# Layers 2 and 3 of a four-layer graph network run as one flow on one Trainium2 core, with the input check's reads of the adjacency moved behind layer 1's end

## The chip, the core and the metric

The kernel runs on one core of a Trainium2 chip (trn2). The metric is the device time of the program in microseconds (us); lower is better. A profile is one more execution, recorded by the hardware; its span is the time between its first and last recorded instruction.

## What is computed

The reference sends 4096 nodes with 64 features each through four graph layers, with a normalisation ahead of each layer and a residual sum behind it. The adjacency matrix is 4096 x 4096, float32, with entries 0 or 1 (an edge with probability about 1/128, and the diagonal). Layer 0 is graph attention with eight heads and an output layer, layer 1 is hyperbolic attention. Cut to what the change touches, the rest is:

```python
h = relu(layernorm(x))                       # ahead of each layer
# layer 2: mean over the neighbours and the node, joined to the node itself
agg = (adj @ h + h) / max(deg + 1, 1)
z = relu(concat([h, agg]) @ W2 + b2)
x = x + z / norm(z)                          # row by row
h = relu(layernorm(x))
# layer 3: the first 100 neighbours of each node, the weight of each halved with its rank
x = x + weights(adj, 100, 0.5) @ (h @ W3) + b3
```

Layer 3's weight of an edge depends on how many edges of the same row stand beside it, so it is built from counts along each row.

## The kernel before, in words

Nodes are held in 32 blocks of 128 (tile `x` and its normalised copy `h`, [128, 32, 64]). A group is four blocks, 512 nodes; there are eight groups and two halves (`hf`) of 2048 target nodes. The edges are kept in DRAM as one byte each (`mask_d`), written earlier, and are streamed as matmul operands.

**Order of instructions.** A tile layer draws the edges between instructions and then orders each engine's queue from an estimate of its own[...]. `in_order()` pins the order inside a block as it is written. `tc.issue_after(i)` makes the instructions of its block that run on `i`'s engine stand behind `i` there; it adds no wait between engines. Loads are issued on SyncE's queue (SP), small ones on GpSimd's (POOL).

**The input check.** The fast path is valid only if every adjacency entry is 0 or 1. `count_odd` (line 946) loads one slab of the float32 adjacency, 128 x 2048 (1 MB, tile `raw`, two buffers), on SP (L949), and VectorE counts its odd entries in one pass (L950). There are 64 such slabs: 16 are counted in layer 0, 12 are traced in layer 2 (L2525) and 36 in layer 3 (L2710, nine for each of four passes). The total decides at the end (L2758 to L2763) whether the general path must be run.

**Layer 1's finish** (`finish_steps`, line 2356) is run for the two halves, interleaved by `side_by_side` (L2506) and pinned. Per half: `pvt` matmuls (L2376) sum layer 1's accumulators by node, VectorE scales them (L2380), then a long chain of VectorE operations on [128, 16, 64] tiles and on [128, 16] scalars, with ScalarE's Square, Sqrt, Tanh and Sqrt between, the residual, the normalisation (`norm_steps`), and `h` split into two half-precision parts (`HH`, L2497 to L2502).

**Layer 2.** For each half of targets, eight loads of edges (`m2`, 1 MB, three buffers) feed 16 `nacc` matmuls each (features, L2517) and 16 `dc` matmuls (degrees, L2529). At the half's end the sums are copied out (`ev`, `cf`) and four groups are finished one after another (L2552 to L2594): `pnf`, `cat`, transposes and `cT`, `pz`, `zt`, norm, residual. PSUM: five banks for sums, three for the rest. The groups of half 0 stand beside half 1's products.

**Between the layers** `layernorm_relu()` (L2597) normalises the two halves. Then layer 3's pools are opened and its constants made (L2604 to L2650: loads of W3 and b3, the triangle `tri`, `blk`, `late` from the counts, and the scaled weights), and the values `SS` (L2652 to L2666) of the eight groups: transposes, `hT`, `psup`, two half-precision parts.

**Layer 3** makes four passes (`u`) over 1024 targets each. A pass has 32 steps `j`: two `pv` matmuls with `blk` and `late` (L2691), two with `tri` and the edges (L2699), ScalarE's conversion to the weights `w3b` (L2708), and two `sacc` matmuls with `SS` (L2673), one step behind. Every four steps an edge tile `m3` (0.5 MB, three buffers, L2684) is loaded. A pass ends with `ev` (L2717, one on VectorE and one on ScalarE), `pn` (L2722) and the output. `sacc` has two banks, so the next pass's sums start once `ev` has read them.

Of the kernel before, what the change touches and what calls it, by code (L numbers as in the profile page):

```python
# [15 lines left out]
I16 = mybir.dt.int16  # L16
# [814 lines left out]
def kernel(  # L831
# [127 lines left out]
    def norm_steps(bs, wide, tag, act=True):  # L959
# [4 lines left out]
        mean = small("ln_mean", nb)  # L964
# [11 lines left out]
        var = small("ln_var", nb)  # L976
# [1379 lines left out]
    def finish_steps(hf, VQ, VT, fold_v, pabs, wide, ps):  # L2356
# [41 lines left out]
        f, rpm = scal("finf"), scal("rpm")  # L2398
        nc.vector.tensor_scalar(f, pm[:, bs], hrow, None, ALU.mult)
        nc.vector.tensor_tensor(f, f, pc[:, bs], ALU.mult)  # L2400
        nc.vector.reciprocal(rpm, pm[:, bs])
        nc.vector.tensor_tensor(g, g, ab, ALU.mult)
        nc.vector.tensor_tensor(xu, xu, g, ALU.subtract)
        nc.vector.tensor_tensor(xu, xu, f, ALU.mult)
        uu, un, arg = scal("uu"), scal("un"), scal("arg")
        nc.vector.tensor_reduce(uu, t, AX.X, ALU.add)
        nc.vector.tensor_tensor(uu, uu, f, ALU.mult)
        nc.vector.tensor_tensor(uu, uu, f, ALU.mult)
# [3 lines left out]
        nc.vector.tensor_scalar(un, un, sqc, None, ALU.mult)  # L2412
        nc.vector.tensor_tensor(arg, rpm, un, ALU.mult)
        nc.scalar.activation(arg, arg, AF.Tanh)
        yield True

        nc.vector.reciprocal(un, un)
        nc.vector.tensor_tensor(arg, arg, un, ALU.mult)
# [5 lines left out]
        nc.vector.tensor_tensor(den, ab, uu, ALU.mult)  # L2424
        nc.vector.scalar_tensor_tensor(den, den, c2, one2, ALU.mult, ALU.add)
# [3 lines left out]
        nc.vector.tensor_scalar(den, den, MIN_NORM, None, ALU.max)  # L2429
        nc.vector.reciprocal(den, den)  # L2430
        nc.vector.tensor_tensor(pp, pp, den, ALU.mult)
        nc.vector.tensor_tensor(pp, pp, den, ALU.mult)
        nc.vector.tensor_scalar(pp, pp, MIN_NORM, None, ALU.max)
        nc.scalar.activation(pp, pp, AF.Sqrt)
        nc.vector.scalar_tensor_tensor(num, uu, cc, one2, ALU.mult, ALU.add)
        nc.vector.tensor_tensor(num, num, den, ALU.mult)
        nc.vector.tensor_tensor(arg, arg, f, ALU.mult)
        nc.vector.tensor_tensor(den, den, pc[:, bs], ALU.mult)
        nc.vector.tensor_tensor(arg, arg, den, ALU.mult)
# [3 lines left out]
        nc.vector.tensor_scalar(pp, pp, maxn, 1.0, ALU.mult, ALU.min)  # L2443
        nc.vector.tensor_tensor(num, num, pp, ALU.mult)
        nc.vector.tensor_tensor(arg, arg, pp, ALU.mult)
# [15 lines left out]
    def layers_fast(es, *sums):  # L2461
# [14 lines left out]


        with ExitStack() as l2:
            lp = l2.enter_context(tc.tile_pool(name="l2f", bufs=1))
            work = l2.enter_context(tc.tile_pool(name="l2fwork", bufs=2))  # L2480
            ps_acc = l2.enter_context(tc.tile_pool(name="ps_nacc", bufs=5, space=PSUM))
            ps = l2.enter_context(tc.tile_pool(name="ps_l2", bufs=3, space=PSUM))
            w2 = lp.tile([2 * D, D], F32, name="w2f")
            nc.gpsimd.dma_start(w2, W2)
            b2t = lp.tile([P, D], F32, name="b2f")
            nc.gpsimd.dma_start(b2t, b2.unsqueeze(0).to_broadcast([P, D]))
            sel = lp.tile([P, NB * O], BF16, name="sel")
            nc.gpsimd.memset(sel, 0.0)
            nc.gpsimd.memset(sel[:, :: O + 1], 1.0)
            HH = lp.tile([P, NB, 2, D], F16, name="HH")  # L2490
            wide = l2.enter_context(tc.tile_pool(name="finwide", bufs=3))

            def nodes(hf):
                yield from finish_steps(hf, *sums, wide, ps)
                bs = halves[hf]
                hs = wide.tile([P, HB, D], F32, name="hs", tag="fat")
                nc.scalar.activation(HH[:, bs, 0, :], h[:, bs], AF.Copy, scale=VALH)  # L2497
                yield True
                nc.vector.scalar_tensor_tensor(
                    hs, h[:, bs], VALH, HH[:, bs, 0, :], ALU.mult, ALU.subtract  # L2500
                )
                nc.scalar.activation(HH[:, bs, 1, :], hs, AF.Copy, scale=LO)  # L2502


            with in_order():
                side_by_side(nodes(0), nodes(1), 2, 10)  # L2506
            for hf in range(2):
                accs = [ps_acc.tile([P, G], F32, name="nacc", tag="nacc") for _ in range(NS)]
                dc = ps_acc.tile([P, G], F32, name="dc", tag="nacc")
                for q in range(NQ):  # L2510
# [13 lines left out]
                    if hf or q >= NQ // 2:  # L2524
                        count_odd(work, next(todo))  # L2525
# [26 lines left out]
                for g in range(NS):  # L2552
                    b0 = hf * HB + g * GB
                    bs = slice(b0, b0 + GB)
                    hg = h[:, bs, :]
                    pn = ps.tile([P, GB, D], F32, name="pnf", tag="misc")
                    for b in range(GB):
                        nc.tensor.matmul(
                            pn[:, b, :],
                            lhsT=ev[:, g, b * P : (b + 1) * P],  # L2560
                            rhs=fold_h,
                            start=True,
                            stop=True,
                        )
                    cat = work.tile([P, GB, 2 * D], F32, name="cat", tag="cat")
                    nc.gpsimd.tensor_copy(cat[:, :, 0:D], hg)
                    nc.vector.scalar_tensor_tensor(
                        cat[:, :, D:], pn, 1.0 / VALH, hg, ALU.mult, ALU.add
                    )
                    nc.vector.tensor_tensor(  # L2570
                        cat[:, :, D:], cat[:, :, D:], over(deg[:, g, :], D), ALU.mult
                    )
                    cT = work.tile([P, G], F32, name="cT", tag="cT")
                    transpose_to(cT, [cat[:, b, :] for b in range(GB)], P, ps, nc.scalar.copy)
                    pz = ps.tile([P, GB, D], F32, name="pz", tag="misc")
                    for b in range(GB):
                        nc.tensor.matmul(
                            pz[:, b, :], lhsT=cT[:, b * P : (b + 1) * P], rhs=w2, start=True, stop=True
                        )
                    zt = work.tile([P, GB, D], F32, name="zt", tag="zt")  # L2580
                    nc.vector.tensor_tensor(
                        zt, pz, b2t.unsqueeze(1).to_broadcast([P, GB, D]), ALU.add
                    )
                    nc.scalar.activation(zt, zt, AF.Relu)
                    sq = work.tile([P, GB, D], F32, name="sq2", tag="sq2")
                    nc.scalar.activation(sq, zt, AF.Square)
                    nrm = small("nrm", GB)
                    nc.vector.tensor_reduce(nrm, sq, AX.X, ALU.add)
                    nc.vector.tensor_scalar(nrm, nrm, 1e-24, None, ALU.max)
                    nc.scalar.activation(nrm, nrm, AF.Sqrt)  # L2590
                    nc.vector.reciprocal(nrm, nrm)
                    nc.vector.tensor_tensor(zt, zt, over(nrm, D), ALU.mult)
                    xg = x[:, bs, :]
                    nc.vector.tensor_tensor(xg, xg, zt, ALU.add)  # L2594


        layernorm_relu()  # L2597
        with ExitStack() as l3:
            lp = l3.enter_context(tc.tile_pool(name="l3f", bufs=1))
            work = l3.enter_context(tc.tile_pool(name="l3fwork", bufs=2))  # L2600
            ps_acc = l3.enter_context(tc.tile_pool(name="ps_sacc", bufs=2, space=PSUM))
            ps = l3.enter_context(tc.tile_pool(name="ps_l3", bufs=2, space=PSUM))
            ps_v = l3.enter_context(tc.tile_pool(name="ps_v", bufs=2, space=PSUM))
            w3 = lp.tile([D, D], F32, name="w3f")  # L2604
            nc.gpsimd.dma_start(w3, W3)
            b3t = lp.tile([P, D], F32, name="b3f")
            nc.gpsimd.dma_start(b3t, b3.unsqueeze(0).to_broadcast([P, D]))
            aft = lp.tile([P, P], F32, name="aftf")
            nc.gpsimd.affine_select(
                out=aft,  # L2610
                in_=ones,
                pattern=[[-1, P]],
                compare_op=ALU.is_gt,
                fill=0.0,
                base=0,
                channel_multiplier=1,
            )

            lat = lp.tile([P, P], BF16, name="lat")
            nc.vector.memset(lat, 0.0)  # L2620
            for q in range(4):
                qs = slice(q * O, (q + 1) * O)
                nc.vector.tensor_copy(lat[qs, qs], aft[qs, qs])

            nc.vector.tensor_scalar(aft, aft, -VBITS, None, ALU.mult)
            tri = lp.tile([P, P], BF16, name="tri")
            nc.vector.scalar_tensor_tensor(
                tri, ident, MAX_NEIGH * VBITS, aft, ALU.mult, ALU.add
            )
# [189 lines left out]
```

## Time and profile before

Three runs: 2236.69, 2244.22 and 2248.63 us, median 2244.22. The profiled execution took 2246.54 us.

| | |
|---|---|
| profiled execution, time | 2246.54 us |
| its span | 2244.6 us |
| PE busy | 1912.7 us, 85% |
| VectorE (DVE) busy | 1749.8 us, 78% |
| ScalarE (ACT) busy | 1599.9 us, 71% |
| moved by DMA | 239.01 MB, mean 106 GB/s |
| layer 1's last product sum on PE, then its finish | ends 1813.0, finish to 1890.8 us |
| layer 2's products, half 0, then half 1 | 1890.8 to 1928.8, then to 1976.5 us |
| first `ev` of layer 3 on DVE, last `ev` | 2091.5 and 2233.5 us |

How to read it: PE is TensorE's matmuls, PEld its weight loads, SPq SyncE's DMA queue. A group names the line, the engine, the operation, output and inputs, shape and count, then busy time and mean duration, then the idle time of that engine ahead of it and who ended it. A table by windows gives for each stretch of the span the busy time and count of instructions of each engine, the clock granted to TensorE as a share of full speed (PEclk), the share of time in which the DMA engines were busy, and the rate. A timeline row is start, duration, engine, line, operation, and in brackets the idle time before it and its releaser.

### The profile page before, as it was taken

The numbers are of one execution on the slowest core, as the hardware profiler recorded it, in microseconds if no ns is written. First come the engines' busy times: TensorE is split into PE (matmuls) and PEld (weight loads), VectorE is DVE, ScalarE is ACT, GpSimd is POOL, SyncE is SP. The second block draws the span as 40 slices with busy tenths as digits, with TensorE's granted clock in tenths as the row PEclk, the third lists the DMA queues.
The fourth block names the chain that finished last, engine by engine and source line by source line (L and its number), as shares of the span: only waits on it lengthen the run. The fifth ranks groups of instructions, "written<-read, shape, count | busy, mean of one in ns | idle before, by whom it ended". The sixth has DMA issues, their size and how long they took to land.

```text
span 2244.6 us, 43714 instructions
## 1 busy us (share of the span) xinstructions
PE 1912.7 (85%) x19229; PEld 872.8 (39%) x19276; DVE 1749.8 (78%) x2128; ACT 1599.9 (71%) x1347; POOL 84.6 (4%) x124
## 2 busy tenths in 40 slices
PE   4989989999999999859992699989999953959998
PEld 3444444444444444424442233333333331434332
DVE  6689989987898899798657889998999868345451
ACT  4668888996898899557753878888888911115666
POOL 1000100100000000001101000000000000000000
PEclk8999999999999999869995799999999966968999
DMA  9945554352111120367540101101110045526883
GB/s 111 183 91 105 91 90 115 124 187 98 44 63 49 40 77 2 123 227 280 191 139 3 32 28 33 33 24 33 33 33 29 24 147 175 186 78 231 297 305 104
DMA packets 117008, 239.01 MB, mean 106 GB/s; under 512 B 11059, under 2 KB 84003, under 8 KB 102051
## 3 DMA queue, kind: packets, MB, share of 16 engines
q1 hardware_dynamic: 101990, 192.92, 25.1%
q0 software_dynamic: 14816, 43.18, 10.9%
q8 instruction: 153, 2.51, 0.5%
q14 instruction: 49, 0.40, 0.1%
HBM read 245.34 MB, written 49.46 MB: 131 GB/s over the span
## 4 chain that ended last, share of the span: by engine, by line
PE 35%; DVE 16%; ACT 5%; DMA 5%; issue 4%; POOL 0%; SPq 0%; DVEq 0%; POOLq 0%; ACTq 0%
PE accj L2280 6%; PE acco L1971 4%; DMA raw<-in_adj_dram 4%; PE pu L2247 3%; PE nacc L2517 3%; DVE raw L950 3%; PE pf L2318 2%; PE pl L2216 2%; DVE at L2269 2%; PE pl L2219 2%; PE accC L1544 2%; ACT sg L2203 1%; DVE at L2274 1%; PE accB L1544 1%; PE ddo L1984 1%
## 5 line engine op out<-in xcount | busy, mean ns | idle before, releaser
L1208 ACT ACTIVATE st<-srow,nt 128x2048 int8<-128x2048 f32 x352 | 682.8, 1994 | 78.3 <-DVE B L1214 77.5
L1214 DVE TENSOR_TENSOR B<-st,mres 128x1024 int32<-128x1024 int32 x256 | 311.7, 1220 | 68.3 <-PE accC L1544 45.1
L1544 PE MATMUL accB<-B,ybh 128*32 128x512 fp8e4 x3072 | 338.9, 384 | 15.6 <-DVE B L1214 15.6
L1544 PE MATMUL accD<-B,ybh 128*32 128x512 fp8e4 x2048 | 301.1, 387 | 23.6 <-DVE h L1660 23.6
L1544 PEld LDWEIGHTS <-ybh 128*32 128x32 bf16 (+1 forms) x6656 | 196.6, 98 | 239.1 <-issue 76.9
L1544 PE MATMUL accC<-B,ycn 128*32 128x512 fp8e4 x2272 | 268.0, 381 | 1.2 <-issue 1.2
L1544 PE MATMUL accC<-mres,ych 128*32 128x512 fp8e4 x2272 | 268.3, 381 | 0.0
L1544 PE MATMUL accL<-B,ybh 128*32 128x512 fp8e4 x1536 | 220.1, 389 | 4.8 <-DVE h L1664 4.7
L2280 PE MATMUL accj<-sg,VQ 128*64 128x512 f32 (+1 forms) x512 | 200.0, 622 | 20.7 <-DVE sg L2321 9.2
L1544 PEld LDWEIGHTS <-ych 128*32 128x32 f16 x4096 | 168.8, 98 | 116.3 <-issue 11.3
L1202 DVE TENSOR_SCALAR st<-srow,nt 128x2048 uint8<-128x2048 f32 x160 | 205.4, 1284 | 2.5
L950 DVE SCALAR_TENSOR_TENSOR raw<-raw 128x2048 f32<-128x2048 f32 x64 | 146.4, 2287 | 69.6 <-DMA raw<-in_adj_dram 69.6
L2280 PE MATMUL acci<-sg,VQ 128*64 128x512 f32 (+1 forms) x512 | 199.4, 622 | 0.0
L2203 ACT ACTIVATE sg<-pl,rb 128x512 f32<-128x512 f32 x256 | 163.4, 684 | 47.7 <-PE pl L2219 32.2
L2708 ACT ACTIVATE w3b<-pv 128x1024 int16<-128x1024 f32 x128 | 131.1, 1024 | 52.2 <-PE pv L2699 51.8
L1208 ACT ACTIVATE st<-srowo,nto 128x1024 int8<-128x1024 f32 x128 | 137.3, 1138 | 40.9 <-DVE B L1214 40.7
L2247 PE MATMUL pu<-XAf,LDf 66*128 66x512 f32 x288 | 146.5, 611 | 9.1 <-DVE at L2254 7.4
L1544 PE MATMUL accC<-C,ych 128*32 128x512 fp8e4 x1824 | 146.4, 389 | 1.9 <-DVE C L1222 1.9
L1222 DVE TENSOR_TENSOR C<-B,mres 128x1024 int32<-128x1024 int32 x114 | 139.5, 1225 | 3.6
L1544 PEld LDWEIGHTS <-ycn 128*32 128x32 f16 x2272 | 107.8, 97 | 64.0 <-issue 3.2
L2254 DVE TENSOR_SCALAR at<-pu 128x512 f32<-128x512 f32 x144 | 95.2, 684 | 30.0 <-PE pu L2247 29.3
L2517 PE MATMUL nacc<-m,HH 128*128 128x512 fp8e4 x256 | 60.8, 387 | 61.8 <-ACT HH L2502 61.8
(502 smaller groups left out, 3102.5 us busy)
## 6 DMA issues: line engine op xcount, KB each, us to landing
raw<-in_adj_dram SPq DMA_DIRECT2D x64, 1024.0 KB, 6.7
mo<-edges SPq DMA_DIRECT2D x32, 512.0 KB, 4.7
noedge<-nmo POOLq DMA_DIRECT2D x32, 512.0 KB, 4.9
nm<-noedge SPq DMA_DIRECT2D x64, 256.0 KB, 3.0
m<-edges SPq DMA_DIRECT2D x16, 1024.0 KB, 4.8
m<-edges SPq DMA_DIRECT2D x32, 512.0 KB, 5.1
srow<-srow_d SPq DMA_DIRECT2D x15, 1024.0 KB, 6.6
mres<-in_adj_dram POOLq DMA_DIRECT2D x8, 1024.0 KB, 36.3
```

The costliest lines, as they stand in the source:

```text
L950: nc.vector.scalar_tensor_tensor(raw, raw, 0.0, raw, ALU.is_gt, ALU.not_equal, accum_out=bad[:, c : c + 1])
L1202: nc.vector.tensor_scalar(st[:, i, :].bitcast(U8), srow, negs[:, i : i + 1], EDGE, ALU.is_gt, ALU.mult)
L1208: nc.scalar.activation(st[:, i, :], srow, AF.Sign, bias=negs[:, i : i + 1], scale=-1.0)
L1214: nc.vector.tensor_tensor(B.bitcast(I32), st.bitcast(I32), edges.bitcast(I32), ALU.bitwise_and)
L1222: nc.vector.tensor_tensor(C.bitcast(I32), B.bitcast(I32), edges.bitcast(I32), ALU.bitwise_xor)
L1544: ins = nc.tensor.matmul(acc[k * O : (k + 1) * O, :], lhsT=values, rhs=moving(k), start=start, stop=stop,)
L2203: tc.keep_in_program_order(nc.scalar.activation(*args, **kw))
L2247: nc.tensor.matmul(pu, lhsT=LD[:, j * P : (j + 1) * P], rhs=XA[:, grp(gi)], start=True, stop=True,)
L2254: nc.vector.tensor_scalar(at[:, b, :], pu, UMIN, None, ALU.max)
L2280: nc.tensor.matmul(acc[r : r + n, :], lhsT=XQ[:, src, cols], rhs=w, start=start, stop=stop)
L2517: nc.tensor.matmul(accs[k], lhsT=HH[:, j].rearrange("p s d -> p (s d)"), rhs=m8[:, t, k * G : (k + 1) * G], start=(j == 0), stop=(j == NB ...
L2708: nc.scalar.activation(w, pv, AF.Relu)
```

## The change

It has five parts.

1. Layers 2 and 3 share pools, opened ahead of both; the shared PSUM pool `ps` has two banks and layer 2's sums six. Layer 3's loads of W3 and b3 are issued with layer 2's, and its constants are made behind layer 1's finish.
2. A group goes from layer 2's end on through its own normalisation and to its layer-3 values in one function. `late` is made for each half as soon as its groups are through; layer 3's passes follow without a stage between.
3. `count_odd` is traced 3 and 5 times in layer 2 and 7, 11, 11 and 11 times in layer 3. The counts of layer 2 stand behind layer 1's finish on VectorE, those of layer 3 behind the last group's values.
4. `finish_steps` has fewer operations on [128, 16] tiles: the factors `f`, `f2`, `kp`, `pf` and `ac2` are made once in layer 1's stage, and one clamp and several products are folded. The ScalarE steps stay.
5. `norm_steps` names its small tiles by width.

```diff
-        with ExitStack() as l2:
...
-            ps_acc = l2.enter_context(tc.tile_pool(name="ps_nacc", bufs=5, space=PSUM))
-            ps = l2.enter_context(tc.tile_pool(name="ps_l2", bufs=3, space=PSUM))
+        ps = es.enter_context(tc.tile_pool(name="ps_l23", bufs=2, space=PSUM))
...
+        ready, valued = [], []
...
+            ready.append(
                 nc.vector.scalar_tensor_tensor(
                     hs, h[:, bs], VALH, HH[:, bs, 0, :], ALU.mult, ALU.subtract
                 )
+            )
...
+        def not_before_nodes():
+            return tc.issue_after(ready[-1].ins)
+
+        with not_before_nodes():
...
+            blk = lp.tile([P, NB, P], BF16, name="blk")
+            nc.vector.tensor_scalar(blk, over(bsel, P), -VBITS, None, ALU.mult)
...
+        def layer2_group(b0, part, deg):
...
+            nc.vector.tensor_tensor(xg, xg, zt, ALU.add)
+
+            for _ in norm_steps(bs, work, "sq2"):
+                pass
+            hT = work.tile([D, G], F32, name="hT3", tag="hT3")
+            transpose_to(hT, [h[:, b, :] for b in range(b0, b0 + GB)], D, ps, nc.scalar.copy)
+            pu = ps.tile([P, GB, D], F32, name="psup", tag="misc")
...
+            nc.scalar.copy(SS[:, bs, 0, :], pu)
+            lo = work.tile([P, GB, D], F32, name="lo3", tag="lo3")
+            valued.append(nc.vector.tensor_tensor(lo, pu, SS[:, bs, 0, :], ALU.subtract))
+            nc.scalar.activation(SS[:, bs, 1, :], lo, AF.Copy, scale=LO)
...
+        with tc.tile_pool(name="ps_nacc", bufs=6, space=PSUM) as ps_acc:
             for hf in range(2):
...
-                    if hf or q >= NQ // 2:
-                        count_odd(work, next(todo))
+                    if q <= NQ // 2 if hf else q > NQ // 2:
+                        with not_before_nodes():
+                            count_odd(work, next(todo))
...
                 for g in range(NS):
...
+                    layer2_group(hf * HB + g * GB, ev[:, g, :], deg[:, g, :])
                 pl = ps.tile([P, G], F32, name="plate", tag="misc")
                 nc.tensor.matmul(pl, lhsT=lat, rhs=cnt16[:, hf], start=True, stop=True)
                 nc.vector.tensor_scalar(late[:, hf], pl, VBITS, None, ALU.min)
...
-        layernorm_relu()
...
-                        if j % 7 < 2 and j < 28 or j == 30:
-                            count_odd(work, next(todo))
+                    if j % 3 == 0 if u else j % 2 and j > NB // 2 + 1:
+                        with tc.issue_after(valued[-1].ins):
+                            count_odd(work, next(todo))
```

## The prediction

> **What bounds the kernel now.** I read the page's slices first: PE is at 0.8 or more in most of the 40, and the low ones that this change touches are the 33rd, 34th and 36th (1796 to 2020 us). Then the chain of work that ended last, in order of time, and a table by windows cut where that chain changes hands.
>
> ```profile
> core 0: us, PE busy (x) PEld busy (x) DVE busy (x) ACT busy (x) POOL busy (x), PEclk, DMA share, GB/s
> ...
> 1815.00:1830.00 15.00, 13.67 (x64) 13.51 (x64) 4.11 (x10) 0.00 (x0) 0.00 (x0) 0.52 0.82 342
> 1830.00:1890.00 60.00, 0.00 (x0) 0.00 (x0) 56.98 (x98) 12.36 (x16) 0.74 (x2) 0.50 0.52 175
> 1890.00:1929.00 39.00, 38.22 (x258) 15.10 (x259) 16.55 (x38) 5.49 (x8) 0.00 (x0) 0.95 0.53 189
> 1929.00:1977.00 48.00, 47.35 (x344) 23.96 (x342) 17.08 (x41) 7.58 (x18) 2.22 (x5) 1.00 0.37 132
> 1977.00:2005.00 28.00, 19.34 (x88) 16.97 (x88) 10.46 (x30) 6.25 (x15) 1.41 (x3) 0.54 0.00 0
> 2005.00:2025.00 20.00, 0.63 (x1) 0.14 (x2) 15.20 (x26) 2.75 (x6) 2.68 (x3) 0.50 0.50 187
> ...
> 2053.00:2092.00 39.00, 36.40 (x177) 13.10 (x179) 19.57 (x21) 28.46 (x32) 0.00 (x0) 1.00 0.86 294
> 2092.00:2143.00 51.00, 47.95 (x205) 16.18 (x209) 25.20 (x27) 33.26 (x33) 1.55 (x2) 0.90 0.83 295
> ...
> 2190.00:2234.00 44.00, 41.83 (x193) 13.69 (x197) 7.28 (x12) 32.33 (x32) 1.86 (x3) 1.00 0.34 117
> ```
>
> From 1830 to 1890 (layer 1's finish) DVE is the bound, 57 of 60 us. From 1890 to 1977 (layer 2's products) it is PE. From 1977 to 2025 PE works little and at half clock. Layer 3's passes are PE's again, but up to 2190 with the DMA engines busy 83 to 86% of the time; the last pass, which has almost no slabs to load, takes 44 us and the pass from 2092 took 51.
>
> The slabs (`raw`) show why. First the view of that tile, then the timeline of DVE:
>
> ```profile
> DMA to landing us min/median/max: 5.0/6.7/14.1
> ```
>
> ```profile
> 2061.11 2.29 DVE L950 SCALAR_TENSOR_TENSOR raw<-raw 128x2048 f32<-128x2048 f32 x1 [3.78 <-DMA raw<-in_adj_dram]
> ...
> 2070.29 2.29 DVE L950 SCALAR_TENSOR_TENSOR raw<-raw 128x2048 f32<-128x2048 f32 x1 [4.40 <-DMA raw<-in_adj_dram]
> ...
> 2080.30 2.29 DVE L950 SCALAR_TENSOR_TENSOR raw<-raw 128x2048 f32<-128x2048 f32 x1 [3.91 <-DMA raw<-in_adj_dram]
> ```
>
> These are every second count, one of the two buffers: 2.3 us on DVE, then at once the next load, about 7 us. Two buffers turn every 9 to 10 us.
>
> **The change part by part.** Times are from the profiled execution. The order of the built program's instructions says where each stands.
>
> *Layer 1's finish*, 1815.2 (last `VT` sum on DVE) to 1890.8: 75.6 us. In the new order 20 of the 32 `pvt` stand among the last pair products, and of the three groups that stand last on PE one doesn't need the last sum. A group takes 1.7 us now, at half clock (eight passes of 0.214 us). Behind the last sum remain two groups and one scaling, 2 x 1.7 + 0.4 = 3.8 us instead of 14.3. Each matmul is recorded as two passes, so the 20 moved ones are 40; at the 0.12 us of the same kind of matmul at full clock (`pnf`, 8 passes in 0.9 to 1.0 us) they are 4.8 us in a stretch where PE is busy 79 to 82%: between 0 and 4.8, I take 2. From there the chain now takes 61.3 us with 12 slab counts at 2.21 us in it, 26.5 us, all of them on a DVE that never stops. They leave. Some hid ScalarE: the count at 1881.9 lay beside Square (1.06 us), others beside Sqrt behind a table load (1.28 us). I rebuilt the chain operation by operation, 1.2 us for a wide one and 0.2 for a narrow one: 12.9 us up to the second half's `V`, 24.1 to the first half's `HH`, 37.0 in all, of which some 3.3 us are waits that come to light and 1.3 are narrow operations saved. Here the Trainium skill speaks against the removal: "ScalarE: Activation LUTs", Rules for kernel authors, says to budget about 2.7 us for every switch of table set. The new order still has five switches. At the row's 1.28 us I get 37; at 2.7 two switches would show and it would be about 40. The row decides. Sum: 2 + 3.8 + 37 = 43 us instead of 75.6, **-33**.
>
> *Layer 2, half 0*: 38 us now. PE's order has one small matmul (L2534) in the fourth quarter that needs `wsq`, and that stands on DVE behind the second half's chain and `blk` (2.2 us). PE reaches it about 42 us after `V`, DVE about 44.5: 3 us, with the nacc products queued behind. The edge loads queue on SP behind the third slab, which waits for the first count; this ends in the same 3 us. Bounds 0 and 6. **+3**.
>
> *From half 1's start to the first `ev` of layer 3*: 1928.8 to 2091.5, 162.7 us now. It consists of half 1 (48), the tail of four groups at half clock (28), the norm and the wait for W3 and the constants (20) and the first pass with values and slab waits (66). In the new kernel a group is one chain. From the rows at 1931 to 1937: `cat` to `sq` 4.8, norm and residual 2.0; with the rows of `ln_mean` and the value steps scaled to a group (0.46 for each [128,256] operation, 0.2 for a narrow one, 0.57 + 0.65 + 1.0 + 0.4 + 0.5 for transposes, `hT`, `psup`, `SS`, `lo`): norm 3.1, values 3.5. That is 13.4 us, and DVE's order has one group wholly behind the other. Half 0's four groups, 54 us, and three or four slab counts that show with 1.5 to 2.3 us each, 8 us in all, end about 62 us after half 1's start; PE has 36.3 of products and 4 x 4.2 of groups beside it, so DVE's chain, not PE, is late. Then `plate`, `pdeg`, `pnf` 2.5 us. Half 1's four groups run beside pass 0: PE's order puts about nine steps of 1.31 us and 3.8 us of the group into each, 15.6 us, and ScalarE's 1.02 us conversions stand between the chain's eight ScalarE operations. The nearest row for that is the present value stage beside pass 0: 4.5 to 5.3 us from transposes to `lo` instead of 3.5, a factor 1.3 to 1.5. On the 9 us of chain that go through PE and ACT this gives 16 to 18 us; I take 16.5, four times 66. Bounds 13.4 and 22 a group. With two counts (4.6) that stand ahead of `ev`: 62 + 2.5 + 66 + 4.6 = 135. **-27.5**. Norm, W3 and constants are in here at nothing: they lie beside half 0 and the chain.
>
> *From the first to the last `ev`*: 142 us now. Here the slabs come back. Of 48 slabs behind layer 0, 8 are counted in layer 2; DVE's order has two ahead of the first `ev`, then 11, 16 and 11. So 38 slabs instead of 23 fall into three passes, and none of them can start earlier, because both buffers are full while the chain of groups runs. Bytes: 38 x 1.049 + 21 x 0.524 + 1 = 51.8 MB. Between 2091.5 and 2198.6 the DMA queues now move 32.5 MB, 303 GB/s, so 171 us. By buffer turns: a slab landed in 5.0 us when no edge loads ran beside it (1851.6 to 1856.7) and about 7.0 with 1.75 edge loads per turn; with one per turn 6.1, and 2.4 for the count: 19 turns of 8.5 are 162. I take 167. Passes 1 to 3 on PE need 44 each, 132, and are covered. The skill's "DMA: Bandwidth & Descriptors", Bandwidth, gives 341 GB/s for transfers of 1 MB; by that it would be 152. The rows with two slabs in flight decide. **+25**.
>
> *End*: `ev` to the last record 11.1; the flag now stands ahead of the last `ev` on DVE and waits for POOL 0.5: **+1**.
>
> Sum: -33 + 3 - 27.5 + 25 + 1 = -31.5. The profiled execution's 2246.5 becomes 2215; it lay 2.3 above the median of the runs, so the forecast is **2213 us**. A difference under 0.5% (11 us) can hardly be told from none in this kernel.
>
> **The rivals.** *The transfers keep up*: if slabs land in 5 us beside edge loads too, three passes are PE's 132 to 140 us and the gain is 60: about 2183. For it: bins of over 400 GB/s, and the present passes were partly held by SP waiting for PE. Against it: 83 to 86% busy at 300 GB/s. 20%.
>
> *The group chain is slower in company*: 22 us a group, with ScalarE's and PE's queues in strict order, +22 us, and the finish uncovers 5 us more: 2240. For it: factor 1.5 above. 17%, half of it above 2233.
>
> *Slower than before*: SP's edge loads wait for PE to free a tile, slabs stand behind them, counts stand ahead of `ev` on DVE, and `ev` holds PE's next sums. If this ring runs in turn and not side by side, each of three pass ends costs PE's first four or five load periods of 5.24 us, some 20 us: +60, 2273. It decides from about 14 us per pass end (31.5 + 11 over three). Seen now: a pass with ten slabs takes 51 and 48 us instead of 44, so 4 to 7. Against it: six slabs stand on SP ahead of the first load that needs the new pass. 8%.
>
> *That the counts only move* and nothing else is won is inside the sum: -26.5 in the finish, +25 in the passes; the gain must come from the tail and the norm.
>
> **Numbers.** Likeliest case 55%, its own range 2192 to 2232; rivals 20, 17 and 8. The range 2180 to 2241 takes in the first rival's point and most of the second. Faster by over 0.5% (under 2233): 0.83; within 0.5%: 0.09; slower: 0.08.
>
> **What would show it.** No `raw` between 1815 and `HH`; half 0 starting near 1858; clock 1.0 throughout from there to the end of pass 0; the last `lo` near 2030; slab counts with a period of 4.2 to 4.5 us and DMA share over 0.85 from there to the end, PE idle in pass 2 (16 slabs, 68 us against 44). Wrong if the passes take 45 us each, if groups in pass 0 take over 20 us, or if slabs are counted before the last `lo`.

## The result, and the profile after

The changed kernel takes 2209.1 us (median of four runs, 2205.8 to 2209.8) against 2242.6 us of the kernel before (median of four, 2236.7 to 2248.6): a ratio of 0.9848, 95% interval 0.9819 to 0.9877, or 33 us saved. The forecast was 2213. The profiled execution took 2209.57 us, its span is 2207.8: 37 us less than the profiled execution before.

To see where the time went, all profiles are cut at the same five events: the start of the last `VT` sum on DVE, the first `nacc` of layer 2 on PE, half 0's `ev` on DVE, the first and the last `ev` of layer 3 on DVE, and the end of the span. Times per stage in us:

| kernel | finish | half 0 | half 0's `ev` to first `ev` of layer 3 | first to last `ev` | end |
|---|---|---|---|---|---|
| before | 76.3 | 36.6 | 164.1 | 142.0 | 11.1 |
| after | 39.4 | 39.1 | 138.4 | 166.7 | 9.6 |
| difference | -36.9 | +2.5 | -25.7 | +24.7 | -1.5 |

The change wins 63 us in two stages and pays 27 back in two others. The table by windows of the kernel after, in the columns that the prediction showed (busy time and count of PE, PEld, DVE, ACT, POOL, then granted clock, share of busy DMA engines, GB/s):

```profile
1815.00:1854.00 39.00, 2.00 (x16) 1.86 (x16) 31.34 (x68) 13.08 (x16) 2.85 (x7) 0.54 0.49 174
1854.00:1894.50 40.50, 39.16 (x259) 15.38 (x260) 27.57 (x48) 4.98 (x9) 0.00 (x0) 0.94 0.64 236
1894.50:1949.00 54.50, 52.34 (x380) 28.06 (x380) 28.36 (x62) 13.40 (x32) 3.34 (x5) 1.00 0.61 231
1949.00:2031.50 82.50, 73.59 (x354) 34.75 (x355) 31.37 (x80) 49.59 (x77) 1.41 (x3) 0.86 0.18 55
2031.50:2086.00 54.50, 47.39 (x222) 16.77 (x222) 31.35 (x35) 32.52 (x33) 1.56 (x2) 0.97 0.88 308
2086.00:2152.00 66.00, 50.51 (x208) 16.31 (x208) 36.15 (x35) 32.63 (x34) 1.49 (x2) 0.90 0.89 312
2152.00:2198.00 46.00, 41.45 (x189) 12.87 (x187) 26.34 (x26) 32.00 (x32) 1.75 (x3) 1.00 0.86 308
```

Row 1 is the finish: DVE has 68 instructions left, and 31 us of them. Row 4 is the groups of half 1 beside pass 0: the DMA engines are idle there (share 0.18). Rows 5 to 7 are passes 1 to 3: PE is busy 41 to 51 us of 46 to 66, the DMA engines 86 to 89%. The slabs on DVE's timeline, after:

```profile
2062.91 2.29 DVE L950 SCALAR_TENSOR_TENSOR raw<-raw 128x2048 f32<-128x2048 f32 x1 [3.59 <-DMA raw<-in_adj_dram]
...
2071.92 2.29 DVE L950 SCALAR_TENSOR_TENSOR raw<-raw 128x2048 f32<-128x2048 f32 x1 [3.96 <-DMA raw<-in_adj_dram]
```

The counts come in pairs; these are the first ones of two pairs (the second ones, not shown, wait under 0.5 us), and they stand 9.0 us apart. The view of the tile says how long a slab is on its way:

```profile
DMA to landing us min/median/max: 5.0/7.0/15.8
```

7.0 and 2.3 are 9.3: the time of a pair is about the turn of one buffer, load and count. Over the three passes it is somewhat shorter: 38 slabs, 19 pairs, in 166.7 us are 8.8 us a pair.

The slabs reach PE through SyncE's queue. An edge load stands there behind slab loads, and a slab load goes out when a count has freed its buffer (the counts end at 2089.9 and 2092.8 us here):

```profile
2089.96 3.18 SPq L949 DMA_DIRECT2D raw<-in_adj_dram  x2
2093.23 0.52 SPq L2668 DMA_DIRECT2D m<-edges  x1
```

In pass 2 there are two slab loads to each edge load, so the edges come at the pace of the slabs, every 8.3 us, where PE needs new ones every 5.24. What PE waited for in passes 1 to 3 (from 2031 to 2184 us; us in total, times, longest):

```profile
PE pv L2683 <- DMA m<-edges: 13.4, 10, 2.8
PE sacc L2657 <- ACT w3b L2692: 11.3, 22, 0.7
```

### The profile page after: what moved, and what is told of

It is laid out like the page before. It is cut to its first block, busy times and chain, and to the rows that moved or that the text cites. A ratio compares the mean times of both kernels' runs of the same rounds, so it can differ in the third digit from the quotient of the medians.

```text
span 2207.8 us, 43777 instructions
## 1 busy us (share of the span) xinstructions
PE 1907.8 (86%) x19276; PEld 862.1 (39%) x19276; DVE 1753.9 (79%) x2151; ACT 1600.9 (73%) x1359; POOL 84.4 (4%) x124
## 3 DMA queue, kind: packets, MB, share of 16 engines
q0 software_dynamic: 14816, 43.18, 11.2%
## 4 chain that ended last, share of the span: by engine, by line
PE 30%; DVE 15%; issue 11%; ACT 6%; DMA 2%; POOL 0%; DVEq 0%; POOLq 0%; ACTq 0%; SPq 0%
PE accj L2280 6%; PE acco L1971 4%; PE pu L2247 3%; PE pl L2216 2%; PE pf L2318 2%; DVE at L2269 2%; PE pl L2219 2%; PE accC L1544 2%; DVE at L2274 1%; PE accB L1544 1%; PE nacc L2606 1%; ACT sg L2203 1%; PE ddo L1984 1%; ACT xt L2203 1%; DMA raw<-in_adj_dram 1%
## 5 line engine op out<-in xcount | busy, mean ns | idle before, releaser
L1544 PEld LDWEIGHTS <-ych 128*32 128x32 f16 x4096 | 169.0, 99 | 116.0 <-issue 10.8
L950 DVE SCALAR_TENSOR_TENSOR raw<-raw 128x2048 f32<-128x2048 f32 x64 | 146.4, 2289 | 82.8 <-DMA raw<-in_adj_dram 82.8
L1222 DVE TENSOR_TENSOR C<-B,mres 128x1024 int32<-128x1024 int32 x114 | 139.6, 1225 | 3.6
L2216 PE MATMUL pl<-nm,noid 128*128 128x512 fp8e4 x256 | 100.6, 393 | 9.3 <-ACT sg L2203 8.9
## 6 DMA issues: line engine op xcount, KB each, us to landing
mres<-in_adj_dram POOLq DMA_DIRECT2D x8, 1024.0 KB, 36.6
```

What stands on the lines that cost most here:

```text
L950: nc.vector.scalar_tensor_tensor(raw, raw, 0.0, raw, ALU.is_gt, ALU.not_equal, accum_out=bad[:, c : c + 1])
L1222: nc.vector.tensor_tensor(C.bitcast(I32), B.bitcast(I32), edges.bitcast(I32), ALU.bitwise_xor)
L1544: ins = nc.tensor.matmul(acc[k * O : (k + 1) * O, :], lhsT=values, rhs=moving(k), start=start, stop=stop,)
L2216: nc.tensor.matmul(pl, lhsT=noid, rhs=nm[:, b, :].bitcast(F8), start=True, stop=False)
```

## The experiments

Every run was compared with runs of the kernel before on the same chip; all ratios are to those, with their 95% interval. The stages of all of them (columns as above, time as median):

| kernel | time | finish | half 0 | to first `ev` | first to last `ev` | end |
|---|---|---|---|---|---|---|
| counts alone (in the kernel before) | 2232.8 | 53.1 | 37.9 | 174.7 | 144.2 | 10.7 |
| bank order alone (in the kernel before) | 2235.4 | 66.7 | 36.6 | 162.7 | 141.1 | 10.8 |
| counts as before | 2240.2 | 61.0 | 44.4 | 177.7 | 131.8 | 10.2 |
| layer 2's counts back | 2206.4 | 60.9 | 39.5 | 130.3 | 154.4 | 11.0 |
| no counts in layer 3 | 2172.3 | 39.4 | 39.1 | 137.0 | 132.2 | 11.2 |
| three slab buffers | 2196.2 | 39.4 | 39.1 | 140.3 | 152.0 | 11.0 |
| counts in groups | 2171.6 | 40.4 | 39.1 | 133.2 | 133.5 | 11.0 |
| counts in groups, three buffers | 2168.0 | 39.4 | 39.1 | 132.9 | 131.8 | 10.0 |
| old narrow operations | 2214.1 | 41.3 | 39.2 | 137.7 | 171.7 | 9.9 |

### Counts alone, in the kernel before

```diff
...
-                    if hf or q >= NQ // 2:
-                        count_odd(work, next(todo))
+                    if q <= NQ // 2 if hf else q > NQ // 2:
+                        with tc.issue_after(ready[-1].ins):
+                            count_odd(work, next(todo))
...
-                        if j % 7 < 2 and j < 28 or j == 30:
-                            count_odd(work, next(todo))
+                        if j % 3 == 0 if u else j % 2 and j > NB // 2 + 1:
+                            with tc.issue_after(valued[-1].ins):
+                                count_odd(work, next(todo))
```

> The kernel before with part 3 alone: the slab counts traced 3 and 5 times in layer 2 and 7, 11, 11, 11 times in layer 3, those of layer 2 behind layer 1's finish, those of layer 3 behind the last group's values. DVE's order has 4 + 4 counts in layer 2, then 9, 10, 10 and 11 ahead of the four `ev` of layer 3. My theory: the finish loses 12 counts and uncovers some 3 us of waits, -24 us; the slabs come back in the passes, but here they may start with pass 0, because the values of all groups stand ahead of it, so only the last pass (11 slabs instead of 2, 44 to 49 us) and pass 0 (9 instead of 7) grow, +5 to +10: about 2226 us. Rival, that moved counts cost as much later as they save (as in the sum of the prediction, -26.5 and +25): 2240 to 2246 us. Second rival, that the counts are the whole gain: 2209 us.

Measured: 2232.8 us, ratio 0.9952 (0.9936 to 0.9969), 10 us saved. Both rivals fall, and my own figure was 7 us too low. The finish lost 23 us, as expected; the later stages gave about 14 back, not 5 to 10. The window of the value stage in this run shows a part of that:

```profile
1996.00:2038.00 42.00, 40.78 (x136) 23.05 (x137) 6.11 (x19) 15.92 (x30) 0.00 (x0) 0.50 0.05 14
2038.00:2077.00 39.00, 37.85 (x170) 11.80 (x168) 20.04 (x17) 28.43 (x29) 0.00 (x0) 0.96 0.81 292
```

The values of eight groups ran at half clock for 42 us, with the DMA engines idle, and the nine slabs held behind them set the end of pass 0 (39 us for nine, 4.3 each). In the kernel before, six counts ran beside the values, at a clock of 0.75 (2025 to 2057 us): the hold had moved counts out of a stretch that had room for them. How much of the loss is that and how much the clock is not shown.

### Counts as before, in the changed kernel

```diff
-                    if q <= NQ // 2 if hf else q > NQ // 2:
-                        with not_before_nodes():
-                            count_odd(work, next(todo))
+                    if hf or q >= NQ // 2:
+                        count_odd(work, next(todo))
...
-                    if j % 3 == 0 if u else j % 2 and j > NB // 2 + 1:
-                        with tc.issue_after(valued[-1].ins):
-                            count_odd(work, next(todo))
+                    if j % 7 < 2 and j < 28 or j == 30:
+                        count_odd(work, next(todo))
```

> The changed kernel with the counts traced as in the kernel before (12 in layer 2, 36 in layer 3, nothing held behind anything). DVE's order now has 16 counts in layer 1's finish, 3 in half 0, 29 among the groups, and none behind the first `ev` of layer 3. My theory: finish +33 (16 x 2.28 less 3.3 of waits that are covered again), passes 1 to 3 at PE's 44 us each, -33, and the chain of groups lengthened by 10 to 30 us, since DVE is idle for some 75 us of the 137 us there but a count that waits for its slab holds the chain behind it: 2220 to 2240 us. Rival, that holding the counts is neutral and the flow is the whole gain: 2203 to 2215 us. Second rival, that the counts fit into DVE's idle time of the groups without delay: finish +33, passes -33, so the same 2209 us with quite another table of stages.

Measured: 2240.2 us, ratio 0.9993 (0.9974 to 1.0012): no gain at all over the kernel before, at the upper end of what I expected. Both rivals fall. Against the changed kernel, finish and half 0 take 27 us more, the groups 39 more, the passes 35 less. In this run's windows, the groups of half 1 and then pass 1:

```profile
1979.00:2095.70 116.70, 83.86 (x361) 43.13 (x361) 75.44 (x126) 51.43 (x82) 3.93 (x4) 0.72 0.61 211
2095.70:2139.40 43.70, 43.64 (x208) 14.53 (x206) 2.20 (x5) 32.05 (x33) 1.55 (x2) 1.00 0.30 92
```

With the slabs gone from it, a pass is PE's (43.6 of 43.7 us). But the 21 counts between half 1's end and the first `ev` stretched the groups there from 84 to 116 us, though DVE idled 41 us of that. Waits for slabs are 7.7 us of it. PE lost its clock as well (0.72, against 0.86). How the 32 us divide between the places of the counts, the landing of slabs and the clock is not shown.

That a count can hold what stands behind it can be seen in the trace of the kernel before. ScalarE began its `ev` of pass 0 at 2088.19, so the sums were complete; DVE's `ev` stood behind a count that waited for its slab:

```profile
2089.24 2.29 DVE L950 SCALAR_TENSOR_TENSOR raw<-raw 128x2048 f32<-128x2048 f32 x1 [2.53 <-DMA raw<-in_adj_dram]
...
2091.46 0.69 DVE L2717 COPY ev<-sacc 128x512 f32<-128x512 f32 x1
```

So neither the flow alone (-3 us, not told from none) nor the counts alone (-10) is the gain: together they give 33.

### Layer 2's counts back, layer 3's held

```diff
-                    if q <= NQ // 2 if hf else q > NQ // 2:
-                        with not_before_nodes():
-                            count_odd(work, next(todo))
+                    if hf or q >= NQ // 2:
+                        count_odd(work, next(todo))
...
-                    if j % 3 == 0 if u else j % 2 and j > NB // 2 + 1:
+                    if j % 3 == 0 if u else j > NB - 4:
```

> The changed kernel with layer 2's counts as before (12, held behind nothing) and the 36 of layer 3 still held behind the last group's values (3, 11, 11, 11). DVE's order has 12 counts in layer 1's finish again, none in layer 2, 2 ahead of the first `ev` of layer 3 and then 11, 12 and 11. My theory, that holding the counts of layer 2 is about neutral in the new flow (each costs 2.2 us in the finish and 4.4 us in the passes once these are bound by the slabs): finish +24, half 1 and its groups -3 to -8 without counts, passes 34 x 4.4 = 150 instead of 167: 2208 to 2216 us. Rival, that the hold behind the finish carries the 31 us between the changed kernel and the run with the old places: 2232 to 2242 us.

Measured: 2206.4 us, ratio 0.9837 (0.9795 to 0.9879), the same as the changed kernel's 0.9848 (0.9819 to 0.9877). The finish, whose chain holds 12 counts again, took 21.5 us more; 8.1 came back in the groups, which have no layer-2 counts now, and 12.3 in the passes. So holding layer 2's counts is worth nothing that can be told here; what the run with the old places lost against this one, it lost by layer 3's counts, 21 of which ran among half 1's groups.

### No counts in layer 3

```diff
-                            count_odd(work, next(todo))
+                            c = next(todo)
+                            nc.vector.memset(bad[:, c : c + 1], 0.0)
```

> The changed kernel with the 40 slabs that are traced in layer 3 neither loaded nor counted (a store of zero to the count's column stands in their place): this part of the input check is left out. My theory, that the passes 1 to 3 are bound by the slabs and no longer by PE: first to last `ev` from 167 to 132 to 138 us, and 4.6 us of two counts ahead of the first `ev` gone: 2168 to 2178 us. Rival, that the ring of PE, ScalarE's conversions and edge loads takes over 50 us for a pass anyway: 2190 to 2205 us.

Measured: 2172.3 us, ratio 0.9682 (0.9641 to 0.9723). Passes 1 to 3 take 44.1 us each; the window of the first:

```profile
2030.60:2074.70 44.10, 44.04 (x208) 14.57 (x206) 2.26 (x6) 32.58 (x34) 1.56 (x2) 1.00 0.30 91
```

PE is busy 44.04 of 44.10 us. The slabs make the passes 34.5 us longer in the changed kernel; part of that is PE's own work, 139.6 us there and 131.2 here, at a granted clock of 0.95 and 1.00. The rival ring of PE, conversions and edge loads costs nothing without the slabs.

### Three slab buffers

```diff
-        raw = pool.tile([P, HW], F32, name="raw", tag="raw", bufs=2)
+        raw = pool.tile([P, HW], F32, name="raw", tag="raw", bufs=bufs)
```

with `bufs` 3 in layers 2 and 3, and 2 in layer 0.

> The changed kernel with three buffers instead of two for the slabs of layers 2 and 3. If the passes are bound by the bytes (51.5 MB moved in 166.7 us, 309 GB/s, queues busy 86 to 89% of the time): a third slab fills the gaps of the queues, at most 167 x 0.12 = 20 us and probably a third of that, 2200 to 2206 us. If they are bound by the turn of two buffers (landing about 6.4 us and a count of 2.3 us for two slabs, DVE idle for 2 to 5 us ahead of every second count): three slabs a turn, and passes 1 to 3 go down to PE's 44 to 46 us each, 2180 to 2188 us.

Measured: 2196.2 us, ratio 0.979 (0.9748 to 0.9833). Neither forecast holds: the passes take 152 us, 15 less. The windows of passes 1 to 3:

```profile
2032.00:2088.00 56.00, 43.38 (x189) 13.69 (x188) 36.51 (x37) 30.03 (x30) 1.56 (x2) 0.91 1.01 387
2088.00:2136.00 48.00, 44.54 (x210) 14.90 (x208) 27.24 (x27) 33.03 (x34) 1.49 (x2) 1.00 0.89 336
2136.00:2184.00 48.00, 43.83 (x206) 14.70 (x204) 27.62 (x29) 33.05 (x34) 1.86 (x3) 1.00 0.65 246
```

Now pass 1 has the DMA engines busy all the time, at 387 GB/s. The 308 to 312 GB/s of the changed kernel were therefore not the rate of the queues but what two buffers ask of them: the bound was the turn. With it loosened, the bytes bind in pass 1; in pass 3 the DMA engines are free again a third of the time. What holds passes 2 and 3 at 48 instead of 44 us is in PE's waits (2088 to 2184 us):

```profile
PE sacc L2657 <- ACT w3b L2692: 7.5, 13, 0.7
```

No edge load is waited for any more. At some new edge tiles of this kernel and of the changed one, PE's order has four `tri` products of two steps in a row, and the conversion behind them comes late; without the slabs PE's order has no such place in pass 2. So these 7 us belong to the order that the tile layer drew, not to the landing of slabs; no run changed that order alone.

### Counts put into the groups' own waits

The prediction held that no slab could be counted earlier, because both buffers are full while the chain of groups runs. DVE's waits there can be seen in the trace of the changed kernel (one group of half 1, behind `cat` and behind the normalised `h`):

```profile
1983.40 0.42 DVE L2558 TENSOR_TENSOR cat<-cat,degf 128x256 f32<-128x256 f32 x1
1986.56 0.42 DVE L2567 TENSOR_TENSOR zt<-pz,b2f 128x256 f32<-128x256 f32 x1 [2.74 <-PE pz L2563]
...
1993.23 0.43 DVE L981 SCALAR_TENSOR_TENSOR h<-h,ln_var 128x256 f32<-128x256 f32 x1
1997.52 0.42 DVE L2557 SCALAR_TENSOR_TENSOR cat<-pnf,h 128x256 f32<-128x256 f32 x1 [3.86 <-PE pnf L2552]
```

A group has one wait of 2.7 and one of 3.9 us, each long enough for a count. The edit puts one count into each, 16 in all, 4 into half 0, none beside half 1's products otherwise, and 28 into passes 1 to 3 (one of these runs ahead of the first `ev`). With two buffers:

```diff
+            joined = nc.vector.tensor_tensor(cat[:, :, D:], cat[:, :, D:], over(deg, D), ALU.mult)
+            with tc.issue_after(joined.ins):
+                counted = count_odd(work, next(todo), 2)
...
+            with tc.issue_after(counted.ins):
+                nc.vector.tensor_tensor(zt, pz, b2t.unsqueeze(1).to_broadcast([P, GB, D]), ALU.add)
...
+            with tc.issue_after(normed[-1].ins):
+                counted = count_odd(work, next(todo), 2)
...
+                    if u and j % 3 == 0 and j < 30 - 3 * (u > 1):
```

> The changed kernel with two slab counts put into each group, at the two places where DVE waits for PE and ScalarE in the trace (behind the joined `cat`, ahead of `zt`; behind the group's normalisation, ahead of `lo`): 4 counts in half 0, 16 in the groups, 28 in passes 1 to 3 (11, 10 and 7 between the `ev` in DVE's order instead of 11, 16 and 11). My theory: a count of 2.3 us lies inside waits of 3 to 6 us and has over 5 us for its slab to land, so the groups lose 0 to 10 us in all, and the passes go to 45 to 50 us each (about 4.3 us a slab), 145 instead of 167: 2183 to 2195 us. Rival, that any count among the groups lengthens their chain as in the run with the old places (39 us for 29 counts): groups +21, passes -22, 2209 us.

> The same placement with three slab buffers. If both costs are as I hold (the turn of two buffers bounds a slab at 4.3 us, three buffers reach 387 GB/s, that is 2.7 us a slab): passes at PE's 44 to 45 us, groups not longer: 2172 to 2182 us, near the time without any layer-3 slabs. If the two gains are the same gain: the same as the better of the two alone.

Measured: 2171.6 us with two buffers, ratio 0.9685 (0.966 to 0.971), and 2168.0 with three, ratio 0.9677 (0.9661 to 0.9693). Both beat the changed kernel, by 38 and 41 us, and both by more than I expected; with all slabs counted they are as fast as the run that left 40 of them out (2172.3). The same stretch of a group, with two buffers:

```profile
1977.64 0.41 DVE L2560 TENSOR_TENSOR cat<-cat,degf 128x256 f32<-128x256 f32 x1
1977.97 2.29 DVE L950 SCALAR_TENSOR_TENSOR raw<-raw 128x2048 f32<-128x2048 f32 x1
...
1980.80 0.42 DVE L2572 TENSOR_TENSOR zt<-pz,b2f 128x256 f32<-128x256 f32 x1 [0.53 <-PE pz L2567]
...
1987.47 0.42 DVE L983 SCALAR_TENSOR_TENSOR h<-h,ln_var 128x256 f32<-128x256 f32 x1
1987.81 2.28 DVE L950 SCALAR_TENSOR_TENSOR raw<-raw 128x2048 f32<-128x2048 f32 x1
...
1991.75 0.42 DVE L2559 SCALAR_TENSOR_TENSOR cat<-pnf,h 128x256 f32<-128x256 f32 x1 [1.65 <-PE pnf L2554]
```

The waits shrink to 0.5 and 1.7 us, and none of the counts among the groups waits for its slab. From one `cat` row to the corresponding `cat` row of the next group of half 1 it is 14.8 us in both kernels, and from half 0's `ev` to its last `lo` 63 us against 66: the 16 counts cost the groups nothing. So a count among the groups need not cost its 2.3 us; it depends on where it stands. The same kernel kept PE's clock (0.98 in the groups' stretch, 0.72 in the run with the old places), so place and clock are not told apart in that comparison. With three buffers the passes are PE's alone (131.8 us; without any slabs they were 132.2), but the two kernels' intervals overlap, so the third buffer's own worth is not told apart here.

### Bank order alone, in the kernel before

```diff
-            ps_acc = l2.enter_context(tc.tile_pool(name="ps_nacc", bufs=5, space=PSUM))
             ps = l2.enter_context(tc.tile_pool(name="ps_l2", bufs=3, space=PSUM))
+            ps_acc = l2.enter_context(tc.tile_pool(name="ps_nacc", bufs=5, space=PSUM))
```

> The kernel before with one edit: layer 2's PSUM pool of three banks is opened ahead of the one of five sums, so that layer 1's `pvt` finds a bank that is free earlier; on PE 16 of the 32 `pvt` then stand among the pair products. My theory: the stretch from the last `VT` sum to the first `xv` goes from 15 to some 5 us, and the whole by 8 to 12 us, 2231 to 2235 us. Rival: the slab counts fill DVE in the finish, each waits for its load, and the finish ends no earlier: 2240 to 2245 us.

Measured: 2235.4 us, ratio 0.9972 (0.9959 to 0.9984), 5 us saved by the medians and 6 by the ratio, less than the 8 to 12 expected; in the profile the finish lost 9.6. From the last `VT` sum to `xv` on DVE, in the kernel before and in this run:

```profile
1814.51 0.69 DVE L2338 TENSOR_TENSOR VT<-VT,accj 128x512 f32<-128x512 f32 x1
...
1829.52 1.22 DVE L2383 TENSOR_TENSOR xv<-h,VQ 128x1024 f32<-128x1024 f32 x1
```

```profile
1819.31 0.68 DVE L2338 TENSOR_TENSOR VT<-VT,accj 128x512 f32<-128x512 f32 x1
...
1823.44 1.22 DVE L2383 TENSOR_TENSOR xv<-h,VQ 128x1024 f32<-128x1024 f32 x1
```

That is 4.1 us instead of 15.0. The stretch from layer 1's first `VT` sum to its last grew from 530.8 to 533.1 us, 2.3 of the 10.9. So the order in which two pools are opened decides whether PE can start `pvt` early. That it does so through the bank that `pvt` gets is the reading from the program; the edit changes nothing else.

### Old narrow operations

The body of `finish_steps` is the one before; the factors made in layer 1's stage are still made and not used.

```diff
-        nc.vector.tensor_tensor(arg, un, kp[:, bs], ALU.mult)
+        nc.vector.tensor_scalar(un, un, sqc, None, ALU.mult)
+        nc.vector.tensor_tensor(arg, rpm, un, ALU.mult)
...
```

> The changed kernel with the finish's operations on [128, 16] as before (part 4 undone; the factors made in layer 1's stage are still made and not used). My theory: some 8 narrow operations more for each half at 0.1 to 0.2 us, part of them beside ScalarE's steps: the finish +1 to +3 us, the whole 2210 to 2213 us, hardly to be told from the changed kernel by its time. Rival: they are on the chain all the way and the two reciprocals come to light, +5 or more.

Measured: 2214.1 us, ratio 0.9893 (0.987 to 0.9916). The finish is 1.9 us longer, as expected; the passes took 5 us more, in which nothing was changed. So the time of this run can't size the edit; the stage can.

## Why the prediction was right, point by point

The five stages of the profiled executions sum to -36.9 us, where -31.5 was forecast; most of the difference is the finish.

**Layer 1's finish, -33: measured -36.9.** The mechanism holds for this stage: 12 counts leave, ScalarE's waits come to light, `pvt` moves. The terms that were mis-sized are those of `pvt`: 2 for the pair products was 0.6 (first to last `VT` sum 531.4 us instead of 530.8), and 3.8 behind the last sum was 2.5 (last `VT` sum ended 1815.3, `xv` 1817.9). The chain took 36 us, not 37. Five table loads stand in it, at 1.28 us each; the longest wait of DVE behind one is 1.42 us:

```profile
1834.87 0.17 DVE L2407 TENSOR_TENSOR arg<-un,kp 128x16 f32<-128x16 f32 x1 [1.42 <-ACT un L2405]
```

The 2.7 us a switch of the Trainium skill ("ScalarE: Activation LUTs", Rules for kernel authors) would have made the sum 3 us worse; the row was right. For the whole kernel the 12 counts are worth nothing, as the run with layer 2's counts back shows: what this stage wins by them is paid again in the groups and the passes. The prediction has that in its sum.

**Half 0, +3: measured +2.5.** PE waits for DVE ahead of the small matmul L2534, as forecast, but 1.3 us and not 3:

```profile
1873.57 0.40 PE L2534 MATMUL pm<-wsq,ones 64*128 64x64 f32 x2 [1.29 <-DVE aftf L2523]
```

The first 16 `nacc` took 5.9 us instead of 5.2, which was in no term. That the sum came so near is in part luck.

**Half 0's `ev` to the first `ev` of layer 3, -27.5: measured -25.7.** The sum came out, with shifted parts. Half 0's groups ended 65 us after half 1's start, not 62. Half 1's groups run every 14.8 us, not 16.5, but the first took 19.8, with PE at half clock for most of it (with counts in the groups, at full clock, it took 14.7). The two counts ahead of the first `ev` show with 1.4 us (137.0 us without them, 138.4 with them), not 4.6. "Clock 1.0 throughout" was wrong: 0.86 in that stretch. And its statement that no slab can be taken earlier was a property of the placement, not of the stage.

**First to last `ev`, +25: measured +24.7.** Right in size; of its two workings only the one by turns stands. 19 turns of 8.5 us gave 162; they measure 8.8 on average (8.4 in pass 2, with 16 slabs). The 303 GB/s is no limit: three buffers moved 387. The 341 GB/s of the Trainium skill ("DMA: Bandwidth & Descriptors", Bandwidth; measured there on loads issued from GpSimd) lies between what two and three slabs in flight reached. I had set the two workings beside each other as if they confirmed each other; the rate was only the turn seen from the side of the bytes. That 167, the middle of the two, was met to 1 us is luck.

**The end, +1: measured -1.5.** The flag costs nothing that can be seen.

**The rivals.** *The transfers keep up*: no, DVE waited 82.8 us for slabs (those of layer 0 among them), and without them the passes are 34.5 us shorter. *Groups slower in company*: no, 14.8 us. *Slower by a ring at the pass ends*: no; the passes took 50.8, 67.3 and 48.7 us with 11, 16 and 11 slabs, 4.2 to 4.6 us for each slab. *The counts only move*: true of layer 2's, which can go back at no cost, and untrue of the whole: the same flow with unheld counts is as slow as the kernel before.

## What to carry to other kernels

When background work is moved off a chain, look at what the buffers allow where it lands: a load with two buffers cost about half of (landing + use) here, 4.4 us, although at the 387 GB/s of three buffers its 1.05 MB are 2.7 us, and a stretch in which the DMA engines are idle next to one where they are full is room not used. Work off the path belongs into a wait of the chain that is longer than it, pinned behind the operation that starts the wait, with its data long there (16 counts, no delay); left to the tile layer's own places, 21 counts went with a chain 32 us longer. And measure two parts of a change each alone and together before one is called the gain.

## What was not expected of the hardware

PE's clock fell in a short wait and stayed down under load. In the trace of after, around half 1's end on PE:

```profile
1954.67 1.03 PE L1005 MATMUL tr<-ident,h 128*64 128x128 f32 x4 [5.84 <-DVE h L981]
...
1963.41 1.03 PE L2683 MATMUL pv<-m,tri 128*128 128x512 fp8e4 x2
...
1975.00 0.60 PE L2683 MATMUL pv<-m,tri 128*128 128x512 fp8e4 x2
```

PE waited 5.84 us for a group's normalisation; two `pv` then took 1.03 us, and 0.60 only from about 1975, 20 us later. The granted clock agrees: 0.50 in every stretch of 2 us from 1952 to 1974, 1.00 from 1976. With counts alone it was 42 us at 0.50, PE busy 97% by the records.

The Trainium skill ("TensorE: Matmul & The Clock Gate", What's actually happening) has the fall after an idle window of about 3.4 us and the rise after about 3.4 us of sustained work. A wait of 5.84 us is longer than that; but the clock was at 0.72 already from 1950 to 1952, and the wait had begun at 1948.8. In the trace of before it fell between 1978 and 1981 (0.74), and there PE's longest wait was this one:

```profile
1980.33 1.09 PE L1005 MATMUL tr<-ident,cat 128*128 128x128 f32 x4 [1.07 <-DVE cat L2570]
```

The rise does not agree: in both stretches half-clock work went on for many times 3.4 us. In these three traces the clock came back 3 to 5 us after the last 64-column matmuls (`pz` or `psup`) had ended; whether it is such work that keeps it down was not tried. With counts in the groups, PE's order left work beside that wait, and the clock in the stretch from half 1's end to the first `ev` was 0.98 instead of 0.86. A part of that kernel's gain may come from there, at most the 5 us by which that kernel reached its first `ev` sooner (133.2 against 138.4).
